# Layers 1 and 2 of a fused graph network: GpSimd steps cut in pieces, one mask comparison for two heads, roots and second norms queued later

## The chip, the cores and the metric

The kernel runs on one core of one Trainium2 chip. The time is device microseconds (us) of one execution; the smaller the better. TensorE (PE) multiplies matrices and loads a stationary operand before each product (PEld), VectorE (DVE) and ScalarE (ACT) do elementwise work, GpSimd (POOL) does elementwise work off to the side, and SyncE (SP) starts the transfers. Every engine has one queue of its own and takes its instructions strictly in that order, so an instruction that waits holds up all that stand behind it on the same engine.

## What is computed

Four graph layers on 3125 nodes of 128 features and 103,125 edges, each of the form x = layernorm(x + layer(x)). Layer 0 is a weighted neighbour sum with a ReLU. The two layers that the change touches are these:

```
# layer 1: attention over edges with 4 heads of 32 features
h = (x @ W).reshape(n, HEADS, C)
e = leaky_relu(a_s[src] + a_d[dst], 0.2); m = segment_max(e, dst); p = exp(e - m[dst])
out = segment_sum(h[src] * (p / segment_sum(p, dst)[dst]), dst)
out = out + gat_bias + x @ skip_W + skip_b
x = layernorm(x + layernorm(out) * ln_g + ln_b)
# layer 2: attention with one head
e = sum(Q[receiver] * K[sender]) * scale; w = exp(e - segment_max(e))
x = layernorm(x + (segment_sum(w * V[sender]) / segment_sum(w)) @ Wo)
```

Layer 3 is two mean-aggregating layers with a sigmoid.

## The kernel before, in words

**Dense counts.** The first third of the kernel turns the edge list into a dense table of edge counts (`ctd`, 25 blocks of 128 source nodes by 3200 destinations, bf16). All later layers are matrix products with that table. The 3125 nodes are 25 blocks of 128.

**Layer 1, the main loop.** The destinations are cut into four groups, `IG`, of 6, 7, 6 and 6 blocks; the heads are taken two at a time (`hp` is 0 or 2); inside, `c` runs over the 25 source blocks. One (group, hp, c) is an item; there are 200. I call the 25 items of one (group, hp) a half. For an item, TensorE needs the counts `ct` (a transfer of one source block by n destination blocks) and for each of two heads a mask `cm`: the counts where the leaky ReLU of the edge score is on its positive branch, zero elsewhere. For each of the n destination blocks there is one product with the counts (L1297) and one per head with the mask (L1302), 3n in all, summed over c in n PSUM banks.

**The masks.** `masks` (L1262 on) makes a mask in one of two ways. One in five is one VectorE instruction (L1280), a comparison times the counts with a float32 input. The others are a ScalarE activation into a tile `fm` (L1286: ReLU of the scaled score) and a VectorE minimum with the counts into `cm` (L1287). `fm` has 5 buffers, `cm` 8, `ct` 6. The masks of item x+2 are issued in step x.

**The order of the work around it.** A list of due times, filled by `later(k, f)`, places the rest: `step()` runs at the start of every item and issues whatever has come due, so "k items later" is a place in the engines' queues and not a time. The compiler's planner then orders each engine's queue by that order, its own estimate of costs, and free buffers. At the end of a half, `sums` adds up the three parts of each bank on VectorE (L1321), and GpSimd does four multiplications and additions on the result (L1327 to L1330); 4 items later (7 in the first group) `quotients` divides (L1337 to L1343). After both halves of a group, `finish1` is a chain: `norm1` (statistics on VectorE, L1021 to L1025, and the root on ScalarE, L1026), an item later `norm2` (scale, L1035, on ScalarE), three long GpSimd operations on all n blocks (L1082 to L1084: times ln_g, plus ln_b, plus x), 5 items after that the second `norm1`, an item later its `norm2`, and an item later `turns`: for each block, two items apart, a TensorE transposition (L1044), a copy, a product for layer 2 (L1048), and its evacuation (L1049 on ScalarE, L1050 on VectorE). This chain runs beside the next group's first half. When the destinations of a query group are done, `bound2` takes a maximum over all nodes by way of TensorE (L1002, L1013). `skips` adds the skip connection block by block, one per item, from item 2 of a group's first half (L1310, L1311).

**Layer 2.** Two query groups of 13 and 12 blocks by 25 sources: a score product (L1445), an exponential (L1448, ScalarE), a product with the counts (L1449, VectorE) and a sum (L1453, TensorE). The chain of the last group of layer 1 runs beside its first items with shorter distances, and `finish2` normalises after the first query group.

## Time and profile before

| what | value |
|---|---|
| time before, median of 3 runs | 1503.28 us (1501.07 to 1508.55) |
| the profiled execution's own time | 1507.44 us |
| its span in the trace | 1505.6 us |
| layer 1's main loop, first to last product | 540.3 to 948.7 us, 408.4 us |
| busy in that stretch: PE, PEld | 370.13, 353.98 us |
| busy in that stretch: DVE, ACT, POOL | 350.90, 323.23, 93.04 us |
| one `fm` activation (128x768), mean | 926 ns |
| one `cm` minimum (128x768), mean | 640 ns (median without GpSimd beside it 550 ns) |
| one `cm` comparison on VectorE alone (128x768), mean | 1079 ns |
| one long GpSimd operation (128x768), L1082 | 1989 ns mean, 1807 ns least |

The span is what the profiler sees from the first to the last instruction of the program; the device time of the same execution is 1.8 us longer. In the answers that list instructions in order of time, a row has the start, the duration (of several merged instructions, from the first start to the last end), the engine, the line, the operation, its output and inputs, and in brackets how long the engine had been idle before it and which instruction released it. In the table by stretches, "(x230)" is the number of instructions that began in it.

### The profile page before, as it was taken

To read this page: it belongs to the slowest core of one execution; us is meant where nothing else is said; L and a number is where in the kernel's file an instruction comes from. 1 tells how busy PE (TensorE), PEld (TensorE's weight loads), DVE (VectorE), ACT (ScalarE), POOL (GpSimd) and SP (SyncE) were. 2 spreads that over 40 slices of the span, in tenths; PEclk is the share of its full clock that TensorE was granted. 3 is DMA by queue.
4 is the path that set the end of the run, shared out by engine and by line. 5 is a ranking of instruction groups with operands and counts; after the bars stand their busy time and mean duration, and the time that the engine had idled before them with its cause. 6 is when DMAs were issued, how large, how long until landed. Compare 5 with 4: busy or idle time off the path is not lost.

```text
span 1505.6 us, 34986 instructions
## 1 busy us (share of the span) xinstructions
PE 1395.4 (93%) x14775; PEld 1227.3 (82%) x14775; DVE 978.8 (65%) x1575; ACT 914.3 (61%) x1865; POOL 128.9 (9%) x164
## 2 busy tenths in 40 slices
PE   3889999999998988998979989899999999999996
PEld 3889999999998878987978989677777774458996
DVE  4989899999991389898888879534464352012005
ACT  2978789888882489878867787454555331023005
POOL 1000000000000012132032113200000000000000
PEclk8999999999999999999999999999999999999998
DMA  7368789989887733443433534332222218512551
GB/s 206 96 179 226 198 221 242 234 213 230 238 218 221 222 115 114 125 124 113 135 90 112 142 88 117 115 121 70 69 60 81 71 47 309 200 53 114 197 174 46
DMA packets 209700, 223.91 MB, mean 149 GB/s; under 512 B 72956, under 2 KB 183339, under 8 KB 209277
## 3 DMA queue, kind: packets, MB, share of 16 engines
q1 hardware_dynamic: 208748, 218.51, 50.6%
q8 instruction: 117, 1.92, 0.5%
q0 software_dynamic: 400, 1.97, 0.4%
q10 hardware_dynamic: 385, 1.11, 0.2%
q14 instruction: 50, 0.41, 0.1%
HBM read 157.19 MB, written 64.36 MB: 147 GB/s over the span
## 4 chain that ended last, share of the span: by engine, by line
PE 72%; DVE 11%; ACT 8%; DMA 4%; issue 2%; POOL 2%; SPq 0%; ACTq 0%; DVEq 0%; POOLq 0%
PE wp L919 10%; PE acc L1302 9%; PE acc L1453 9%; PE s L1445 8%; PE acc L1553 7%; PE acc L1629 6%; PE acc L820 6%; PE acc L1297 5%; PE cp L911 3%; DVE cm L1287 3%; ACT wod L882 3%; PE left L820 2%; DMA cw<-wd 2%; ACT fm L1286 1%; DVE cm L1280 1%
## 5 line engine op out<-in xcount | busy, mean ns | idle before, releaser
L1302 PE MATMUL acc<-vp,cm 128*128 128x198 bf16 x2500 | 344.5, 252 | 8.2 <-DVE cm L1287 6.7
L1297 PE MATMUL acc<-vp,ct 128*128 128x204 bf16 x1250 | 317.1, 255 | 10.1 <-DVE vp L1205 4.5
L1286 ACT ACTIVATE fm<-adr,bas 128x768 bf16<-128x768 f32 (+1 forms) x320 | 287.2, 953 | 61.9 <-DVE cm L1287 60.1
L1302 PEld LDWEIGHTS <-cm 128*128 128x128 bf16 x2500 | 236.4, 98 | 25.2 <-DVE cm L1287 8.8
L919 PE MATMUL wp<-wod,ohc 128*128 128x128 bf16 x3768 | 239.6, 220 | 7.1 <-ACT cs L924 5.4
L919 PEld LDWEIGHTS <-ohc 128*128 128x128 bf16 x3768 | 220.9, 99 | 8.7 <-issue 8.3
L876 DVE TENSOR_TENSOR wod<-ohd,w 128x4096 bf16<-128x4096 bf16 (+2 forms) x122 | 221.4, 1867 | 0.4 <-PE wp L919 0.4
L1287 DVE TENSOR_TENSOR cm<-fm,ct 128x768 bf16<-128x768 bf16 (+1 forms) x320 | 202.6, 664 | 28.8 <-PE acc L1302 13.9
L882 ACT ACTIVATE wod<-ohd,wu 128x128 bf16<-128x128 bf16 x628 | 197.7, 397 | 0.0
L1449 DVE TENSOR_TENSOR e<-e,ct 128x416 f32<-128x416 f32 (+1 forms) x175 | 108.0, 623 | 110.4 <-ACT e L1448 102.8
L1448 ACT ACTIVATE e<-s,f_nm 128x416 f32<-128x416 f32 (+1 forms) x175 | 109.6, 633 | 103.1 <-PE s L1445 95.7
L1453 PEld LDWEIGHTS acc<-self__8043,e 128*128 128x128 f32 x1250 | 148.2, 192 | 19.8 <-issue 18.9
L820 PE MATMUL acc<-f_xw,cw 128*128 128x128 f32 x1000 | 147.8, 289 | 11.9 <-DMA cw<-wd 11.9
L1453 PE MATMUL acc<-self__8043,e 128*128 128x129 f32 x1250 | 148.5, 276 | 0.0
L1445 PE MATMUL s<-yT,f_xT 128*128 128x416 f32 (+1 forms) x350 | 143.1, 544 | 4.5 <-ACT rt L1425 2.6
L820 PEld LDWEIGHTS acc<-f_xw,cw 128*128 128x128 f32 x1000 | 127.7, 198 | 12.5 <-DMA cw<-wd 12.5
L1297 PEld LDWEIGHTS <-ct 128*128 128x128 bf16 x1250 | 122.1, 98 | 4.0 <-issue 2.7
L924 ACT CAST cs<-cp 128x500 bf16<-128x500 f32 x157 | 90.7, 578 | 39.5 <-PE cp L911 39.5
L1445 PEld LDWEIGHTS s<-yT,f_xT 128*128 128x128 f32 x350 | 62.5, 191 | 55.4 <-issue 40.7
L865 DVE TENSOR_TENSOR ohd<-kd,ramp 128x4096 bf16<-128x4096 bf16 (+1 forms) x41 | 90.1, 2200 | 20.3 <-PE cp L911 18.6
L930 ACT COPY ws<-wp 128x512 f32<-128x512 f32 x157 | 90.2, 579 | 20.9 <-PE wp L919 20.6
L911 PE MATMUL cp<-ohc,ohd 128*128 128x125 bf16 x1256 | 96.3, 220 | 3.7 <-ACT ws L930 3.5
(341 smaller groups left out, 1520.6 us busy)
## 6 DMA issues: line engine op xcount, KB each, us to landing
ct<-f_ctd SPq DMA_DIRECT2D x46, 800.0 KB
wd<-ws SPq DMA_DIRECT2D x39, 896.0 KB
cw<-wd SPq DMA_DIRECT2D x50, 640.0 KB
ct<-f_ctd SPq DMA_DIRECT2D x150, 192.0 KB
f_ctd<-cs SPq DMA_DIRECT2D x20, 1000.0 KB
ct<-f_ctd SPq DMA_DIRECT2D x50, 224.0 KB
ct<-f_ctd SPq DMA_DIRECT2D x25, 416.0 KB
ct<-f_ctd SPq DMA_DIRECT2D x25, 365.2 KB
```

The lines of the kernel that those rows point to most:

```text
L820: steps.append(lambda j=j, a=cw[:, j - h, :]: nc.tensor.matmul(accs[j // 4][:, j % 4, :], a, xw[:, i, :], start=False, stop=(i == NB - 1 a ...
L876: tip[s] = nc.vector.tensor_tensor(packed(f, ww), packed(ohd, ww), twos(w2[s])[:, ww], OP.mult)
L882: nc.scalar.activation(wod[2][:, BW + w, :], ohd[:, BW + w, :], AF.Copy, scale=w3[:, 1, at : at + 1])
L911: nc.tensor.matmul(cp[:, j, 0:KW], ohd[:, w, :], ohc[:, w, 0:KW], start=(j == 0 and q == 0), stop=(j == 3 and q == 1), skip_group_check=True,)
L919: made = nc.tensor.matmul(wp[:, j, :], ohc[:, w, :], wod[s][:, w, :], start=(j == 0 and q == 0 and s == 0), stop=(j == 3 and q == 1 and s ...
L1286: nc.scalar.activation(f[:, : n * P], at, AF.Relu, bias=bas[:, c, h : h + 1], scale=UP)
L1287: nc.vector.tensor_tensor(m[:, : n * P], f[:, : n * P], ct[:, : n * P], OP.min)
L1297: nc.tensor.matmul(out_(F1, PW), ct[:, k * P : (k + 1) * P], vp[:, c, hp : hp + 2, :, 2 * F1 : V1], start=(c == 0), stop=False, skip_group ...
L1302: nc.tensor.matmul(out_(0, 2 * F1)[:, j], ms[j][:, k * P : (k + 1) * P], vp[:, c, hp + j, :, 0 : 2 * F1], start=False, stop=(c == NB - 1 a ...
L1445: nc.tensor.matmul(s[:, :m], xT[:, c * P : (c + 1) * P], yT[:, i0 * P + a : i0 * P + a + m], start=True, stop=True)
L1448: nc.scalar.activation(e[:, a : a + m], s[:, :m], AF.Exp, bias=nm[:, q : q + 1], scale=scale)
L1453: nc.tensor.matmul(acc[k // 3][:, (k % 3) * (P + 1) : (k % 3 + 1) * (P + 1)], es[q, c][:, k * P : (k + 1) * P], vo[:, c, 0 : P + 1], start ...
```

## The change

Six things are done, all in layers 1 and 2.

1. The root (ScalarE's Sqrt) is taken out of `norm1` into `root`, and is issued one item after the statistics; `norm2` one item after that. This also holds for layer 2's `finish2`.
2. GpSimd's four steps after `sums`, issued at once before, are due 1, 2, 3 and 4 items later (a copy of the degrees 5), and `quotients` 6 (9) instead of 4 (7). The last half of the last group keeps them at once.
3. The three long GpSimd operations of `finish1` become six, on the first three and the remaining blocks, due an item apart. The second norm comes 8 items after the first scale instead of 5, `turns` 3 items after the second scale instead of 1. The last group issues the pieces at once, with the second norm 2 items later.
4. `bound2`'s transposition is due 3 items after its maximum and the rest 3 items after that, for the first query group. `skips` starts at item 5 instead of 2.
5. Both heads' masks of an item are in one tile `cm` (6 buffers, each twice as large; `fm` is gone). Where c % 5 == 2 both are made by VectorE alone. Otherwise ScalarE writes both activations into the tile and one VectorE minimum with the counts, repeated for the two heads, works on it in place.
6. The masks that are issued in the first item of a half get an edge: their VectorE instructions are queued behind the last L1321 of the half before.

```diff
@@ norm1
-        nc.scalar.activation(sd, sd, AF.Sqrt)
         return sp, mv, sd
+
+    def root(state):
+        nc.scalar.activation(state[2], state[2], AF.Sqrt)
@@ bound2
-        d = highest(sp, mq, 1)
-
-        def rest():
+        wait = 1 if q else 3
+
+        def rest(d):
...
-        later(1, rest)
+        def over():
+            d = highest(sp, mq, 1)
+            later(wait, lambda: rest(d))
+
+        if q:
+            over()
+        else:
+            later(wait, over)
@@ finish1
         def first_norm():
             keep["a"] = norm1(sp, r, i0, n)
-            later(gap[0], first_scale)
+            later(gap, lambda: root(keep["a"]))
+            later(gap + 1, first_scale)
+
+        def affine(m):
+
+            j = slice(m // 3 * 3, 3 if m < 3 else n)
+            nj = j.stop - j.start
+            row_ = (g_row, b_row)[m % 3][:, None, :].to_broadcast([P, nj, P]) if m % 3 < 2 else xs[:, j]
+            nc.gpsimd.tensor_tensor(rs[:, j], rs[:, j], row_, OP.mult if m % 3 == 0 else OP.add)
 
         def first_scale():
             norm2(keep["a"], r, r, i0, n)
-            nc.gpsimd.tensor_tensor(rs, rs, g_row[:, None, :].to_broadcast([P, n, P]), OP.mult)
-            nc.gpsimd.tensor_tensor(rs, rs, b_row[:, None, :].to_broadcast([P, n, P]), OP.add)
-            nc.gpsimd.tensor_tensor(rs, rs, xs, OP.add)
-            later(gap[1], second_norm)
+
+            for m in range(6):
+                if g == len(IG) - 1:
+                    affine(m)
+                else:
+                    later(1 + m, lambda m=m: affine(m))
+            later(2 if g == len(IG) - 1 else 8, second_norm)
 
         def second_norm():
             keep["b"] = norm1(sp, r, i0, n)
-            later(gap[0], second_scale)
+            later(gap, lambda: root(keep["b"]))
+            later(gap + 1, second_scale)
...
-            later(gap[0], lambda: turns(0))
+            later(1 if g == len(IG) - 1 else 3, lambda: turns(0))
@@ masks
-        mp = st.enter_context(tc.tile_pool(name="f_mp1", bufs=8))
+        mp = st.enter_context(tc.tile_pool(name="f_mp1", bufs=6))
...
-            ms = []
-            for h in (hp, hp + 1):
-                at = adrs[g, hp][:, h - hp, : n * P]
-                m = mp.tile([P, 7 * P], BF16, name="cm")
-                if (2 * c + h) % 5 == 0:
-                    nc.vector.scalar_tensor_tensor(
-                        m[:, : n * P], at, nas[:, c, h : h + 1], ct[:, : n * P], OP.is_gt, OP.mult
-                    )
-                else:
-
-                    f = mp.tile([P, 7 * P], BF16, name="fm", bufs=5)
-                    nc.scalar.activation(f[:, : n * P], at, AF.Relu, bias=bas[:, c, h : h + 1], scale=UP)
-                    nc.vector.tensor_tensor(m[:, : n * P], f[:, : n * P], ct[:, : n * P], OP.min)
-                ms.append(m)
-            ready_[g, hp, c] = (ct, ms)
+            m = mp.tile([P, 2, 7 * P], BF16, name="cm")
+            if c % 5 == 2:
+                for j in range(2):
+                    made = nc.vector.scalar_tensor_tensor(
+                        m[:, j, : n * P], adrs[g, hp][:, j, : n * P], nas[:, c, hp + j : hp + j + 1], ct[:, : n * P],
+                        OP.is_gt, OP.mult,
+                    )
+            else:
+
+                for j in range(2):
+                    nc.scalar.activation(
+                        m[:, j, : n * P], adrs[g, hp][:, j, : n * P], AF.Relu, bias=bas[:, c, hp + j : hp + j + 1], scale=UP
+                    )
+                made = nc.vector.tensor_tensor(
+                    m[:, :, : n * P], m[:, :, : n * P], ct[:, None, : n * P].to_broadcast([P, 2, n * P]), OP.min
+                )
+            ready_[g, hp, c] = (ct, m)
+            return made
@@ sums
-            nc.gpsimd.tensor_tensor(lo, lo, fbb[1], OP.mult)
-            nc.gpsimd.tensor_tensor(hi, hi, fbb[0], OP.mult)
-            nc.gpsimd.tensor_tensor(hi, hi, lo, OP.add)
-            nc.gpsimd.tensor_tensor(hi, hi, self_[:, i0 : i0 + n, hp : hp + 2, :], OP.add)
+            last = pool is lp
+            for k, (o, y, op) in enumerate((
+                (lo, fbb[1], OP.mult), (hi, fbb[0], OP.mult), (hi, lo, OP.add),
+                (hi, self_[:, i0 : i0 + n, hp : hp + 2, :], OP.add),
+            )):
+                if last:
+                    nc.gpsimd.tensor_tensor(o, o, y, op)
+                else:
+                    later(1 + k, lambda o=o, y=y, op=op: nc.gpsimd.tensor_tensor(o, o, y, op))
...
-            later(1 if last else 4 if g else 7, quotients)
+            later(1 if last else 6 if g else 9, quotients)
@@ the items of layer 1
-            if c == (2 if g else 0) and hp == (0 if g else H - 2):
+            if c == (5 if g else 0) and hp == (0 if g else H - 2):
                 later(0, lambda: skips(i0, i0 + n))
...
-                masks(*items[y_])
+                with ExitStack() as q_:
+                    if c == 0 and summed[0]:
+                        q_.enter_context(tc.issue_after(summed[0].ins))
+                    masks(*items[y_])
@@ finish2
                 keep[h] = norm1(ends[-1], r, *halves[h])
-                later(1, lambda: two(h))
+                later(1, lambda: root(keep[h]))
+                later(2, lambda: two(h))
```

More of the change, by code (lines that the diff above doesn't have):

```diff
@@ L1302, in products @@
                 nc.tensor.matmul(
-                    out_(0, 2 * F1)[:, j], ms[j][:, k * P : (k + 1) * P], vp[:, c, hp + j, :, 0 : 2 * F1],
+                    out_(0, 2 * F1)[:, j], ms[:, j, k * P : (k + 1) * P], vp[:, c, hp + j, :, 0 : 2 * F1],
                     start=False, stop=(c == NB - 1 and j == 1), skip_group_check=True,
@@ L1320, in sums @@
             for k in range(n):
-                nc.vector.tensor_reduce(
+                summed[0] = nc.vector.tensor_reduce(
                     nz[:, k], acc[k][:, 0 : 2 * HW].rearrange("p (h s c) -> p h c s", s=3, c=PW), AX.X, OP.add
@@ L1326, in sums @@
             fbb = [fb[:, s, i0 : i0 + n, hp : hp + 2, None].to_broadcast([P, n, 2, F1]) for s in range(2)]
-            nc.gpsimd.tensor_tensor(lo, lo, fbb[1], OP.mult)
-            nc.gpsimd.tensor_tensor(hi, hi, fbb[0], OP.mult)
-            nc.gpsimd.tensor_tensor(hi, hi, lo, OP.add)
-            nc.gpsimd.tensor_tensor(hi, hi, self_[:, i0 : i0 + n, hp : hp + 2, :], OP.add)
+            last = pool is lp
[7 more added lines that the diff above has]
+                    later(1 + k, lambda o=o, y=y, op=op: nc.gpsimd.tensor_tensor(o, o, y, op))
             if hp == 0:
-                nc.gpsimd.tensor_copy(deg[:, i0 : i0 + n], nz[:, :, 0, 2 * F1])
-            last = pool is lp
+                later(5, lambda: nc.gpsimd.tensor_copy(deg[:, i0 : i0 + n], nz[:, :, 0, 2 * F1]))
             def quotients():
@@ L1344, in quotients @@
                 if hp == H - 2:
-                    later(1 if last else 3, lambda: finish1(ends[-1], g, (1, 1) if last else (1, 5)))
-            later(1 if last else 4 if g else 7, quotients)
+                    later(1 if last else 3, lambda: finish1(ends[-1], g, 1))
+            later(1 if last else 6 if g else 9, quotients)
         ends.append(sp)
+        summed = [None]
         acc = None
```

## The prediction, made before the change was run

> **What bounds the kernel now.** I read the page's shares first, then the table by stretches, then who waited for whom, then the time order around the worst places.
>
> ```profile
> PE 1395.4 (93%) x14775; PEld 1227.3 (82%) x14775; DVE 978.8 (65%) x1575; ACT 914.3 (61%) x1865; POOL 128.9 (9%) x164
> PEclk8999999999999999999999999999999999999998
> ```
>
> TensorE is the bound over the whole; what can be won in layer 1 is only time in which it doesn't run at its pace. The table by stretches gives the pace and the room:
>
> ```profile
> 720.00:740.00 20.00, 20.00 (x230) 20.00 (x229) 14.88 (x23) 17.61 (x19) 0.00 (x0) 1.00 0.47 128
> 780.00:800.00 20.00, 13.57 (x121) 12.44 (x122) 13.94 (x40) 14.59 (x27) 2.29 (x2) 0.83 0.20 54
> 880.00:900.00 20.00, 15.87 (x135) 14.26 (x136) 14.37 (x39) 16.49 (x31) 1.37 (x1) 0.83 0.26 70
> ...
> 540.30:948.70 408.40, 370.13 (x3907) 353.98 (x3908) 350.90 (x701) 323.23 (x451) 93.04 (x83) 0.97 0.40 113
> ```
>
> The columns are PE, PEld, DVE, ACT, POOL busy, then the granted clock. Undisturbed, 230 products run in 20 us, 87 ns each: an item of 18 takes 1.57 us, of 21 1.83 us. In layer 1 PEld is busy 353.98 of 408.40 us, so at most 54 us can be won. I counted the loads item by item and subtracted pace and the other lines' loads: 52 us too long in all. Of these, 20.6 lie in three places (around 686, 780 and 883, two items each: 3.8, 9.6 and 7.2), 18.1 in the first seven items of the seven later halves, 10.4 in the first half, and the rest is scattered. Two of the three places are the two stretches with a clock of 0.83. Most items in the second part of a half are at pace to 0.1 us.
>
> What happens at 780, in order of time:
>
> ```profile
> 775.57 2.09 POOL L1082 TENSOR_TENSOR f_xw<-f_xw,f_g_row 128x896 f32<-128x896 f32 x1 [10.50 <-ACT f_xw L1035]
> 776.28 4.14 DVE L1287 TENSOR_TENSOR cm<-fm,ct 128x768 bf16<-128x768 bf16 x2 [1.24 <-ACT fm L1286]
> 777.74 2.27 POOL L1083 TENSOR_TENSOR f_xw<-f_xw,f_b_row 128x896 f32<-128x896 f32 x1
> 780.09 2.28 POOL L1084 TENSOR_TENSOR f_xw<-f_xw,f_x 128x896 f32<-128x896 f32 x1
> 782.40 1.45 DVE L1021 BATCH_NORM_STATS2 bs<-f_xw 128x6 f32<-128x128 f32 x7 [1.97 <-POOL f_xw L1084]
> 785.34 0.21 ACT L1026 ACTIVATE sd<-sd 128x7 f32<-128x7 f32 x1 [3.94 <-DVE sd L1025]
> 787.47 2.79 ACT L1035 ACTIVATE f_x<-f_xw,ms,sd 128x128 f32<-128x128 f32 x7
> 788.00 0.18 PEld L1044 LDWEIGHTS acc<-f_ident,f_x 128*128 128x128 f32 x1 [6.18 <-ACT f_x L1035]
> ```
>
> Three long GpSimd operations run in a row. Two minima take 4.14 us instead of some 1.0: each gets through only when a GpSimd operation has ended. VectorE then stands at the second norm's statistics until L1084 is done, ScalarE at the root behind them, and TensorE at the first transposition of `turns`. All are in-order queues, so masks, activations and products stand behind.
>
> The list of waits shows smaller ones of the same kind, `bound2`'s, and one in layer 2:
>
> ```profile
> PEld L1302 <- DVE cm L1287: 8.8, 9, 3.4
> PEld acc L1044 <- ACT f_x L1035: 6.2, 1, 6.2
> PEld few L1044 <- DVE self__8043 L1050: 5.5, 3, 2.7
> PEld s L1445 <- ACT rt L1425: 3.2, 1, 3.2
> ...
> PE few L1002 <- DVE mq L1058: 1.5, 1, 1.5
> PE acc L1013 <- DVE d_all L1007: 1.5, 1, 1.5
> ```
>
> **The change part by part.**
>
> *Second norm, roots, turns.* The chain from first scale to second norm gets 8 items (12.6 us at 1.57) instead of 5 (7.9). Its work: scales 2.8 (the row of L1035), then GpSimd 2.09 + 2.27 + 2.28 = 6.6 and gaps, 9.7 in all: too long for 5 items, inside 8. The root comes an item behind its statistics (7 L1021, 7 L1023, one L1025: 2.0 us with VectorE undisturbed), so ScalarE can do an item's activations instead of standing 3.9 us. Turns get three items, 4.7 us, for recip, scale and seven L1035 (0.3 + 2.8). The waits of 1.97, 3.94 and 6.18 should all go, and the low clock with them. What is late next: two norms of 2.0 us and the GpSimd pieces, now each some items apart, against a mask lead that I read as 3 to 3.5 us in undisturbed parts. I keep 1 us per place: 20.6 - 3 = 17.6 won. Ends: 0 (the stall moves) and 20.6.
>
> *Pieces.* An L1343 on 384 elements takes 0.95 us (954.81, VectorE quiet), an L1082 on 768 1.81 us: two pieces cost 0.1 us more than one long one, on an engine that is idle nine tenths of the time; no cost while the second norm has its slack of 2.9 us. GpSimd isn't paced by items: its queue holds nothing between the pieces, so they run back to back when their inputs are there. What changes is the grain: with VectorE let through between two operations, a piece of 1 us costs a mask 1 us, not 2.
>
> *Both masks in one minimum.* 160 of 1536 or 1792 elements replace 320. Undisturbed medians are 550 ns at 768 and 618 ns at 896, so 0.53 ns an element and 0.14 us fixed: 0.96 us for 1536. Against two of 0.55 that is 0.14 us less; in runs where rows overlap ("0.93 us x2" in the chain) some 0.03. So 5 to 22 us of VectorE over layer 1, beside TensorE in the steady part. The counts repeated over the middle dimension keep the two-per-cycle rate: L865 reads its `ramp` so and takes 2291 ns for 4096 elements, 0.56 ns each. The comparisons stay 80. An item's masks now wait for both activations, 0.85 us more than for one; the lead covers it. ScalarE writes into a tile that TensorE frees six items later instead of one that VectorE frees: more room, not less.
>
> *Boundaries of halves.* There VectorE does 6 or 7 sums (0.49 us apart), then runs behind with two items of masks ready while four GpSimd steps and two of `quotients` (5 to 8 us) take their turns. With one VectorE operation per GpSimd operation an item costs two GpSimd operations before and one after. Summing minima and comparisons that overlap GpSimd in layer 1 against their undisturbed medians gives 38.5 us lost beside 95 us of GpSimd, 0.40. One step of 0.9 to 1.2 us then costs 0.4 us per item: 0.96 + 0.4 is below 1.57. Of the 18.1 us in these items, `bound2` has 2.9 (its two waits above), which three items of distance remove. Of the other 15.2 I take half, 7 (ends 0 and 12). Item c = 2, two comparisons of 1.0 us, comes straight behind the sums by the new edge; that is in the half I leave. Skips, moved from item 2 to 5, leave this place to masks.
>
> The Trainium skill, page "SBUF — State Buffer", section "SBUF: two separate sides", says that VectorE with two SBUF inputs and GpSimd take a shared pair of ports in turn, as a lock that is kept for the whole instruction. The 4.14 us of two minima beside two GpSimd operations agree in kind. By the rule an item at a boundary would cost 0.96 + 0.95 to 1.2, or 1.9 to 2.2 us, above 1.57, shortening the operations would leave the sum locked the same, and the boundary term would be about 3 instead of 7, the total 4 smaller.
>
> *New costs.* `turns` now run from item 24 of a first half to item 12 of the second, across the boundary, in three groups. Each turn needs VectorE's or ScalarE's copy an item before the masks would. The price seen is 2.3 to 2.7 us for a turn that met the burst (L1044 waiting for L1050). I take 1 us per boundary, 3 in all; ends 0 and 8.
>
> *First half.* VectorE is full there (20.00 of 20.00 in 580 to 600); 20 joint minima save 0.03 to 0.14 each: 1.5 (ends 0.6 and 2.8).
>
> *Layer 2.* The 3.2 us at L1445 come from ScalarE standing at the second norm's root while the copy of the degrees waits behind. With the root an item later, I take 2 (ends 0 and 3.2). The last group's chain ends three or four items later (turns from item 9 instead of 6, the bound at 23 instead of 20); its blocks are needed from item 18 on and the second query group's bound at item 24, so it costs nothing with an item of 5.7 us in hand, and up to 3 us if that is missed. Transfers are the same in number and order; no SP issue moves.
>
> **Sum.** 17.6 + 2.9 + 7 + 1.5 + 2 - 3 = 28. The profiled execution has 1507.44, so 1479.4; the median is 4.2 us below that execution, so 1475; I say 1477.
>
> **The rivals.**
>
> *The stall moves.* VectorE, busy 351 of 408 us, is behind after statistics, pieces and sums alike; spacing them only spreads the wait. For: leads near zero after the GpSimd burst of 664 to 671, where no norm stood. Against: the steady items need 1.2 us of VectorE of 1.57. Price: a third of the first term (6), bound2 2.9, nothing at boundaries, -3: 6 us, so 1497.
>
> *Slower: turns across the boundary.* TensorE's queue is in order, so a transposition that waits for a scale or a copy behind the sums stops the products, and the sums stop too. For: L1044 waits are the largest of layer 1. Against: for groups of 6 two banks alternate. If the first turn in each of three groups costs the 9.6 us of 780 again, all 17.6 are gone; with 2.5 more for two later turns each (15), and the boundary gain of 7 gone, 28 - 17.6 - 7 - 12 is -9: 1512. It decides from about 9 us per boundary on.
>
> *Slower: the joint minimum at one element per cycle.* L1280 rises 1.06 ns per element between its two widths. At that rate a joint minimum takes 1.8 us, an item 1.85 us of VectorE instead of 1.2, above TensorE's 1.57: 200 items by 0.3, about 60 us: 1560. L865 speaks against it.
>
> **How the numbers follow.** My case 0.70 (its own range 1463 to 1492), the moving stall 0.14, turns 0.10, single rate 0.03, others 0.03. Half a percent, 7.5 us, is what this measurement can tell from no change. The moving stall lies half on either side of 1495.8: faster 0.77, same 0.11, slower 0.12. From 1460 to 1508 leaves out the slow rivals and a few percent below.
>
> **What would show it.** Right: no stretch of layer 1 with a clock of 0.83; L1044 waits under 1 us; the statistics no longer released by GpSimd; 160 minima of 0.95 us; main loop near 382 us. Wrong: L1302 waiting for the joint minimum throughout, or L1044 waits in the first items of second halves.

## The result, and the profile after

The changed kernel takes 1514.11 us (median of 11 runs, 1509.02 to 1517.02), the kernel before 1505.27 beside it (11 runs, 1501.07 to 1508.55): a ratio of 1.0052, 95% interval 1.0041 to 1.0062. The forecast was 1477; the change made the kernel 0.5% slower.

The two profiled executions differ by 1.6 us only (1509.02 against 1507.44), because the one of after is the fastest of its runs and the one of before among the slowest. So these two traces show only a part of the loss; where the rest of the 8.8 us lies can't be read from one execution of each. The granted clock of single executions varies too, over the same range in both kernels (0.973 to 0.986); the trace of before has 0.973 and the trace of after 0.986.

The page of after, shares and granted clock:

```profile
PE 1388.8 (92%) x14762; PEld 1218.5 (81%) x14775; DVE 949.0 (63%) x1415; ACT 910.7 (60%) x1865; POOL 134.3 (9%) x176
...
PEclk9999999999999999999999999999999999999998
```

The table by stretches (PE, PEld, DVE, ACT, POOL busy, granted clock, DMA share, GB/s):

```profile
539.10:951.30 412.20, 369.68 (x3907) 350.75 (x3908) 318.76 (x538) 320.51 (x451) 97.35 (x92) 0.98 0.39 112
...
770.00:790.00 20.00, 18.40 (x187) 17.76 (x186) 13.21 (x39) 15.32 (x23) 6.80 (x6) 0.91 0.37 99
780.00:800.00 20.00, 17.98 (x203) 17.49 (x202) 12.69 (x30) 15.57 (x28) 6.80 (x6) 1.00 0.40 107
...
880.00:900.00 20.00, 16.89 (x191) 16.41 (x189) 12.12 (x26) 16.28 (x26) 5.42 (x6) 1.00 0.38 100
```

VectorE is busy 32 us less in the main loop than before (318.76 against 350.90), the two stretches with a clock of 0.83 now have 1.00 (just before the first of them, from 770 to 790, it is 0.91), and the loop is 3.8 us longer (412.2 against 408.4). Less work and a slightly better clock (0.98 against 0.97 over the loop) did not shorten it. The waits show what did the opposite (in total, times, longest, for 520 to 960 us):

```profile
PEld L1326 <- DVE cm L1309: 26.4, 22, 2.9
DVE cm L1309 <- DMA ct<-f_ctd: 24.4, 29, 3.2
...
DVE bs L1021 <- POOL f_xw L1095: 16.8, 6, 3.6
...
DVE rz L1365 <- POOL nz L1359: 12.5, 7, 2.2
ACT sd L1029 <- DVE sd L1025: 12.3, 5, 5.0
...
DVE bs L1021 <- POOL f_xw L1371: 6.9, 4, 2.0
...
DVE rz L1365 <- POOL nz L1357: 1.5, 1, 1.5
...
PEld few L1013 <- DVE d_all L1007: 0.7, 1, 0.7
```

and the same in before:

```profile
DVE bs L1021 <- POOL f_xw L1084: 5.6, 2, 3.6
...
ACT sd L1026 <- DVE sd L1025: 4.2, 2, 3.9
...
DVE bs L1021 <- POOL f_xw L1343: 3.1, 3, 1.4
...
DVE rz L1337 <- POOL nz L1330: 1.5, 1, 1.5
```

VectorE stands for GpSimd 37.7 us (12.5 and another 1.5 at the divisions `rz`, 23.7 at the statistics `bs`); before it was 10.2. ScalarE stands at roots 12.3 us instead of 4.2. TensorE waits 26.4 us for the minima's masks, 8.8 before.

Where in the loop that lands, counted as in the prediction (time per item, less 87 ns a product, less the duration of the other lines' loads; an item runs from its first load to the next item's):

| too long, us | before | after |
|---|---|---|
| first half | 10.4 | 8.2 |
| first seven items of the seven later halves | 18.3 | 38.4 |
| their items 7 to 24 | 24.3 | 10.4 |
| all | 53.0 | 57.0 |

So the three long stalls of TensorE did go, all but a few us (the third row holds them), and the boundaries of the halves took back more than they gave. One boundary of after, VectorE and then GpSimd in order of time:

```profile
697.70 3.46 DVE L1345 TENSOR_REDUCE nz<-acc 128x134 f32<-128x402 f32 x7
701.09 2.92 DVE L1299 SCALAR_TENSOR_TENSOR cm<-adr,nas,ct 128x896 bf16<-128x896 f32 x2
703.93 1.86 DVE L1309 TENSOR_TENSOR cm<-cm,ct 128x1792 bf16<-128x1792 bf16 x1
707.99 0.17 DVE L1365 TENSOR_SCALAR rz<-nz 128x14 f32<-128x14 f32 x1 [2.20 <-POOL nz L1359]
...
708.50 1.07 DVE L1309 TENSOR_TENSOR cm<-cm,ct 128x1792 bf16<-128x1792 bf16 x1
```
```profile
701.25 3.59 POOL L1359 TENSOR_TENSOR nz<-nz,fb 128x462 f32<-128x462 f32 x2 [25.09 <-DVE nz L1345]
704.79 1.05 POOL L1361 COPY f_deg<-nz 128x7 f32<-128x7 f32 x1
705.80 1.00 POOL L1359 TENSOR_TENSOR nz<-nz 128x462 f32<-128x462 f32 x1
706.88 1.08 POOL L1359 TENSOR_TENSOR nz<-nz,self__8043 128x462 f32<-128x462 f32 x1
```

After the sums (L1345) VectorE makes the masks of two items only (two comparisons, one joint minimum). Then the division (L1365) stands in its queue, although the code asks for it 6 items after the sums, and waits 2.20 us until GpSimd's steps end at 707.96. The next minimum stands behind it and runs without a wait of its own once it gets its turn (708.50). Statistics of another group's second norm fare the same at 785 us:

```profile
784.79 0.68 DVE L1021 BATCH_NORM_STATS2 bs<-f_xw 128x6 f32<-128x128 f32 x3 [2.84 <-POOL f_xw L1095]
...
788.72 0.29 DVE L1021 BATCH_NORM_STATS2 bs<-f_xw 128x6 f32<-128x128 f32 x1 [3.03 <-POOL f_xw L1095]
```
```profile
783.76 1.00 POOL L1095 TENSOR_TENSOR f_xw<-f_xw,f_x 128x384 f32<-128x384 f32 x1
...
787.41 1.27 POOL L1095 TENSOR_TENSOR f_xw<-f_xw,f_x 128x512 f32<-128x512 f32 x1
```

VectorE waits for the third and for the sixth piece, 5.9 us together. Counting in VectorE's queue by how many items' masks (of 200) an instruction stands behind: the sums of the first group's second half stand behind 52, their division behind 54, and that group's second norm behind 66. Where the order of the code is kept, as in the run e1_pin below, the same two stand behind 61 and 74. In the kernel before, this norm stood behind 63 and 64; with the order of the code kept (e5_before_pin) it stands behind 68.

### The profile page after: what moved, and what is told of

Read it like the earlier page. It is cut to its first block, busy times and chain, and to the rows that moved or that the text cites. A ratio compares the mean times of both kernels' runs of the same rounds, so it can differ in the third digit from the quotient of the medians.

```text
span 1507.2 us, 34792 instructions
## 1 busy us (share of the span) xinstructions
PE 1388.8 (92%) x14762; PEld 1218.5 (81%) x14775; DVE 949.0 (63%) x1415; ACT 910.7 (60%) x1865; POOL 134.3 (9%) x176
## 4 chain that ended last, share of the span: by engine, by line
PE 69%; DVE 10%; ACT 8%; POOL 5%; DMA 4%; issue 3%; SPq 0%; DVEq 0%; ACTq 0%; POOLq 0%
PE wp L919 10%; PE acc L1485 9%; PE s L1477 8%; PE acc L1326 7%; PE acc L1586 7%; PE acc L1662 6%; PE acc L820 6%; PE acc L1321 4%; PE cp L911 3%; ACT wod L882 3%; POOL nz L1359 2%; DVE cm L1309 2%; PE left L820 2%; DMA cw<-wd 2%; ACT cm L1306 2%
## 5 line engine op out<-in xcount | busy, mean ns | idle before, releaser
L1326 PE MATMUL acc<-vp,cm 128*128 128x198 bf16 x2500 | 341.9, 251 | 22.7 <-DVE cm L1309 20.1
L1321 PE MATMUL acc<-vp,ct 128*128 128x204 bf16 x1250 | 313.9, 254 | 12.2 <-DVE nz L1345 4.2
L1306 ACT ACTIVATE cm<-adr,bas 128x768 bf16<-128x768 f32 (+1 forms) x320 | 283.6, 951 | 43.6 <-PE acc L1326 41.0
L1326 PEld LDWEIGHTS <-cm 128*128 128x128 bf16 x2500 | 233.2, 97 | 47.2 <-DVE cm L1309 26.4
L1309 DVE TENSOR_TENSOR cm<-cm,ct 128x1536 bf16<-128x1536 bf16 (+1 forms) x160 | 166.9, 1050 | 44.1 <-DMA ct<-f_ctd 24.4
L1321 PEld LDWEIGHTS <-ct 128*128 128x128 bf16 x1250 | 121.4, 97 | 4.2 <-issue 3.2
L930 ACT COPY ws<-wp 128x512 f32<-128x512 f32 x157 | 90.1, 577 | 20.1 <-PE wp L919 19.8
L865 DVE TENSOR_TENSOR ohd<-kd,ramp 128x4096 bf16<-128x4096 bf16 (+1 forms) x41 | 90.1, 2200 | 18.3 <-PE cp L911 17.4
```

What stands on the lines that cost most here:

```text
L1306: nc.scalar.activation(m[:, j, : n * P], adrs[g, hp][:, j, : n * P], AF.Relu, bias=bas[:, c, hp + j : hp + j + 1], scale=UP)
L1309: made = nc.vector.tensor_tensor(m[:, :, : n * P], m[:, :, : n * P], ct[:, None, : n * P].to_broadcast([P, 2, n * P]), OP.min)
L1321: nc.tensor.matmul(out_(F1, PW), ct[:, k * P : (k + 1) * P], vp[:, c, hp : hp + 2, :, 2 * F1 : V1], start=(c == 0), stop=False, skip_group ...
L1326: nc.tensor.matmul(out_(0, 2 * F1)[:, j], ms[:, j, k * P : (k + 1) * P], vp[:, c, hp + j, :, 0 : 2 * F1], start=False, stop=(c == NB - 1 a ...
```

## The experiments

My first theory (the queue theory of the expectations): the planner pulls VectorE's dependent steps forward in its queue, ahead of masks, so the distances in items are not kept, and VectorE stands for GpSimd. Rivals: the wider `cm` tiles and the counts' buffers (29.2 us of waits for `ct`, 24.4 of them at the minima), the joint minima, the turns across the boundary. "The edge" below means that what a step issues on VectorE is queued behind the last mask issued before it. All numbers of the runs are in the table; "waits" is VectorE's standing for GpSimd at divisions and statistics between 520 and 960 us. Boundaries (the first seven items of the seven later halves) and rest (their items 7 to 24) are, as above, the time that is too long; loop, boundaries, rest and waits are of one profiled execution each.

Each ratio is against runs of the kernel before on the same chip (medians 1503.86 to 1505.37); loop is first to last product.

| run | median us | ratio, 95% interval | loop us | first half | boundaries | rest | waits us |
|---|---|---|---|---|---|---|---|
| before | 1505.27 | 1 | 408.3 | 10.4 | 18.3 | 24.3 | 10.2 |
| after | 1514.11 | 1.0052 (1.0041 to 1.0062) | 412.1 | 8.2 | 38.4 | 10.4 | 37.7 |
| e1_pin | 1488.31 | 0.9904 (0.9884 to 0.9925) | 390.5 | 9.3 | 18.8 | 7.9 | 6.3 |
| e2_ct7 | 1504.31 | 1.0011 (0.9999 to 1.0022) | 407.9 | 9.7 | 33.9 | 10.0 | 34.3 |
| e3_masks | 1516.75 | 1.0086 (1.0057 to 1.0115) | 421.2 | 9.9 | 30.4 | 25.4 | 27.7 |
| e4_order | 1502.95 | 0.9993 (0.9984 to 1.0003) | 406.2 | 10.1 | 26.7 | 14.5 | 16.4 |
| e5_before_pin | 1503.82 | 0.9999 (0.9984 to 1.0014) | 408.5 | 8.4 | 17.5 | 27.1 | 8.3 |
| e6_order_pin | 1489.71 | 0.9892 (0.9864 to 0.9921) | 393.2 | 8.3 | 22.5 | 7.3 | 4.9 |
| e7_pin_ct7 | 1486.06 | 0.9869 (0.9840 to 0.9897) | 391.0 | 10.9 | 15.3 | 9.8 | 6.3 |
| e8_masks_pin | 1500.04 | 0.9968 (0.9951 to 0.9984) | 404.1 | 10.7 | 11.4 | 26.7 | 8.2 |
| e9_pin_l2 | 1478.93 | 0.9827 (0.9794 to 0.9860) | 390.1 | 9.0 | 16.4 | 9.6 | 1.4 |
| e10_pin_act | 1488.36 | 0.9895 (0.9866 to 0.9923) | 389.7 | 11.1 | 15.1 | 8.8 | 6.3 |
| e11_turns_late | 1483.79 | 0.9867 (0.9841 to 0.9894) | 387.8 | 10.7 | 14.1 | 8.2 | 6.3 |
| e12_pin_norms | 1498.04 | 0.9955 (0.9939 to 0.9971) | 400.7 | 9.7 | 31.7 | 4.5 | 17.3 |
| e13_pin_div | 1496.29 | 0.9944 (0.9928 to 0.9961) | 400.8 | 9.6 | 20.4 | 15.7 | 18.2 |
| e14_far | 1512.42 | 1.0056 (1.0035 to 1.0078) | 417.6 | 9.7 | 43.6 | 8.5 | 31.2 |
| e15_l2_turns | 1478.02 | 0.9822 (0.9806 to 0.9839) | 389.1 | 10.6 | 15.6 | 8.2 | 1.4 |
| e16_cmp1 | 1510.01 | 1.0032 (1.0016 to 1.0049) | 413.9 | 12.8 | 23.3 | 22.8 | 23.4 |
| e17_l2_cmp1 | 1481.89 | 0.9837 (0.9800 to 0.9874) | 393.3 | 8.9 | 22.2 | 7.3 | 0.0 |

### The edge alone, and the counts' buffers alone

e1_pin, the changed kernel with the edge:

```diff
-            step()
+            with ExitStack() as q_:
+                if pinned:
+                    q_.enter_context(tc.issue_after(pinned[-1].ins))
+                step()
...
-                    masks(*items[y_])
+                    pinned.append(masks(*items[y_]))
```

> The changed kernel, with one edge more: the VectorE instructions that a step issues are queued behind the last mask issued before that step, so that the planner can't put them earlier. Queue theory (VectorE's divisions and statistics were placed four to six items before their due step and wait there for GpSimd): VectorE's waits for GpSimd in layer 1's main loop, 38 us in the changed kernel (18.7 + 6.9 at L1021, 14.0 at L1365 less some outside), fall below 8, TensorE's waits for joint minima from 26 to below 10, the main loop from 412 to about 390 to 397, the time from 1514 to 1490 to 1499. Counts theory (masks wait for the transfers of counts, 29 us): waits for counts stay at 25 to 30, the time stays within 4 us of 1514. Turns theory (turns across the boundary of halves): the second halves keep their excess of 10, 4 and 5 us, time 1505 to 1514.

e2_ct7, the changed kernel with another buffer for the counts:

```diff
-        cp = st.enter_context(tc.tile_pool(name="f_cp1", bufs=6))
+        cp = st.enter_context(tc.tile_pool(name="f_cp1", bufs=7))
```

> The changed kernel with 7 buffers of counts instead of 6 (more don't fit), all else as it is. Counts theory: the masks' waits for counts fall from 29 to below 15 us and the time by 5 to 10 us, to 1504 to 1509. Queue theory and turns theory: the waits for counts may fall, but they lie mostly where the masks have a lead of 4 to 5 us; the time stays within 3 us of 1514.

Measured: the edge turns 0.5% slower into 1.0% faster; the loop falls by 21.6 us, the boundaries from 38.4 to 18.8, TensorE's waits for the minima's masks from 26.4 to 10.6 us. The queue theory had forecast this to within 2 us of its ranges. The buffer takes the waits for counts from 29.2 to 1.1 us and wins about 6 us by the ratios, 4.2 us of it seen in the loop; VectorE's standing for GpSimd stays (34.3). So the waits for counts had a price of their own in the changed kernel, as the counts theory said; the queue theory's forecast for this run, within 3 us of 1514, missed. With the edge the waits for counts are as long as without (28.1) and harm little: removing them there (e7_pin_ct7) is not to be told from nothing (the intervals of the two ratios overlap). The same boundary with the edge, VectorE in order of time:

```profile
688.46 3.47 DVE L1345 TENSOR_REDUCE nz<-acc 128x134 f32<-128x402 f32 x7
691.84 2.92 DVE L1299 SCALAR_TENSOR_TENSOR cm<-adr,nas,ct 128x896 bf16<-128x896 f32 x2
694.68 1.86 DVE L1309 TENSOR_TENSOR cm<-cm,ct 128x1792 bf16<-128x1792 bf16 x1
...
696.67 1.84 DVE L1309 TENSOR_TENSOR cm<-cm,ct 128x1792 bf16<-128x1792 bf16 x1
698.44 1.97 DVE L1299 SCALAR_TENSOR_TENSOR cm<-adr,nas,ct 128x896 bf16<-128x896 f32 x1
700.34 1.08 DVE L1309 TENSOR_TENSOR cm<-cm,ct 128x1792 bf16<-128x1792 bf16 x1
...
701.54 1.08 DVE L1309 TENSOR_TENSOR cm<-cm,ct 128x1792 bf16<-128x1792 bf16 x1
702.53 1.14 DVE L1299 SCALAR_TENSOR_TENSOR cm<-adr,nas,ct 128x896 bf16<-128x896 f32 x1
703.60 0.17 DVE L1365 TENSOR_SCALAR rz<-nz 128x14 f32<-128x14 f32 x1
```

Six items of masks (four comparisons, four minima) now lie between sums and division, and the division waits for nothing: it runs 11.7 us after the sums' end instead of 6.8, and the loop is shorter for it.

### Which part of the change costs what, with and without the edge

e3_masks is the kernel before with only the joint masks (parts 5 and 6 of the change):

```diff
+            m = mp.tile([P, 2, 7 * P], BF16, name="cm")
+            if c % 5 == 2:
...
+                made = nc.vector.tensor_tensor(
+                    m[:, :, : n * P], m[:, :, : n * P], ct[:, None, : n * P].to_broadcast([P, 2, n * P]), OP.min
+                )
```

e4_order is the changed kernel with the masks of before in separate tiles, so the distances and pieces without part 5. Part 6, the edge behind the sums, stands in both runs; none has joint masks without it:

```diff
+                    f = mp.tile([P, 7 * P], BF16, name="fm", bufs=5)
+                    nc.scalar.activation(f[:, : n * P], at, AF.Relu, bias=bas[:, c, h : h + 1], scale=UP)
+                    nc.vector.tensor_tensor(m[:, : n * P], f[:, : n * P], ct[:, : n * P], OP.min)
```

> The kernel before with the joint masks alone (one tile of 6 buffers, one minimum for two heads, both comparisons at c % 5 == 2, the edge behind the sums); all distances as before. Queue theory: it is the joint masks that make the planner place the divisions 2 items and the statistics 4 to 8 items behind the sums, so this kernel has VectorE's waits for GpSimd at 30 us or more although VectorE is busy some 30 us less, and is no faster than before: 1503 to 1520. Turns theory: turns are where they were, so the gain of the masks shows: 1485 to 1497. Counts theory: waits for counts of 20 to 30 us as in the changed kernel, 1505 to 1515.

> The changed kernel with the masks of before (two tiles, two minima, fm of 5 and cm of 8 buffers); all distances, pieces, roots and the edge as changed. Queue theory: the planner puts divisions and statistics within an item or two of where they stood in the kernel before, pieces and roots help a little at the second norm: 1495 to 1505. Turns theory: the turns across the boundary cost by themselves: 1507 to 1516. Counts theory: no waits for counts over 5 us, the gain of the distances shows: 1485 to 1497.

e5_before_pin, e6_order_pin and e8_masks_pin are the kernel before, e4_order and e3_masks with the edge of e1_pin; e7_pin_ct7 is e1_pin with the seven buffers of e2_ct7.

> The kernel before with the edge alone: VectorE's instructions of a step stay behind the last mask issued before that step. Nothing else is changed. Queue theory: in the kernel before the planner put divisions and statistics nearly where they were due, so the edge changes little: 1498 to 1507. Rival (the edge is what wins, whatever the distances and masks): 1485 to 1495.

> The changed distances, pieces and roots with the masks of before (two minima an item) and the edge behind the last mask. Queue theory: the distances now hold on VectorE's queue, the second norm no longer waits for GpSimd and the turns not for the norm; VectorE still has its 30 us more of work at the boundaries: 1490 to 1498. Rival (the joint masks carry the gain of the pinned kernel): 1500 to 1506.

> The changed kernel with the edge behind the last mask and 7 buffers of counts. If the waits for counts (28 us on VectorE's queue in the pinned kernel) cost TensorE time there, they fall to below 5 and the time to 1480 to 1485. If they lie where the masks have a lead, the loop stays at 390 us; the time can still fall by up to 5 us, since the stage before layer 1 ended 4 us earlier in the run with 7 buffers: 1483 to 1490.

> The kernel before with the joint masks and the edge behind the last mask; distances as before. Queue theory: the 13 us that the joint masks alone cost go (divisions and statistics are behind their masks again), and the lighter VectorE wins some, but the second norm still stands 5 items behind the first scale and waits for GpSimd's long operations as in the kernel before: 1492 to 1502. Rival (joint masks cost by themselves, by waits for counts or for the second activation): 1508 to 1518.

| median us | without the edge | with the edge |
|---|---|---|
| neither part | 1503.9 | 1503.8 |
| joint masks only | 1516.8 | 1500.0 |
| distances and pieces only | 1503.0 | 1489.7 |
| both | 1514.1 | 1488.3 |

These runs come from more than one chip; the ratios in the large table, each against the same chip, give the same picture. What follows. The edge by itself does nothing for the kernel before. The distances shorten the long stalls (rest 24.3 to 14.5, with the edge 7.3), but without the edge they give most of the gain back at the boundaries (18.3 to 26.7). The joint masks alone make the boundaries 12.1 us worse (30.4) and leave the stalls. The two boundary losses add up: 18.3 + 8.4 + 12.1 = 38.8, and both together measure 38.4. With the edge the joint masks cost nothing any more: at the old distances they win 0.3% (e8_masks_pin against e5_before_pin, boundaries 11.4 against 17.5), at the new ones nothing that can be told (e1_pin against e6_order_pin). The distances win 1.1% with the edge and two minima, 0.6% with the edge and joint ones. So what the joint masks cost is an effect of the queue's order, not of the minimum's speed: a joint minimum is 958 ns in the median, two of before were 553 ns each. What the distances win, they win in the rest: at the boundaries they cost 5.0 us (17.5 to 22.5) and 7.4 us (11.4 to 18.8) even with the edge.

### Divisions or statistics

e12_pin_norms has the edge on the two `norm1` of `finish1` only:

```diff
+            with ExitStack() as q_:
+                if g < len(IG) - 1:
+                    q_.enter_context(tc.issue_after(pinned[-1].ins))
+                keep["b"] = norm1(sp, r, i0, n)
```

e13_pin_div has it on the maximum and the reciprocal of `quotients` only:

```diff
+                with ExitStack() as q_:
+                    if not last:
+                        q_.enter_context(tc.issue_after(pinned[-1].ins))
+                    nc.vector.tensor_scalar(rz, hi[:, :, :, C], 1e-38, None, OP.max)
+                    nc.vector.reciprocal(rz, rz)
```

> The changed kernel with the edge on the statistics of the two norms alone; the divisions of the quotients, the scales' reciprocals and the copies stay where the planner puts them. If the statistics, hoisted ahead of masks, are the whole loss (they wait 16.8 and 6.9 us for GpSimd), the time is 1488 to 1492, as with the edge on everything; if the divisions (12.5 us of waits) carry half of it, 1497 to 1504; if neither is the cause, 1512 or more.

> The changed kernel with the edge on the two VectorE instructions of the quotients (maximum and reciprocal of the sums' weights) alone; statistics and copies stay where the planner puts them. If the loss is the sum of statistics (16 us by the run with the edge on them) and divisions, this run wins the other 10 and stands at 1502 to 1506. If the divisions only hand their wait on to the statistics, it stands at 1511 to 1515. If one of the two places is enough to lead the rest back, 1490 to 1498.

The waits of e12_pin_norms, where line numbers are up to 7 higher:

```profile
DVE rz L1372 <- POOL nz L1366: 12.4, 7, 2.2
...
DVE bs L1022 <- POOL f_xw L1099: 2.0, 1, 2.0
...
DVE bs L1022 <- POOL f_xw L1378: 1.4, 1, 1.4
```

and of e13_pin_div:

```profile
DVE bs L1021 <- POOL f_xw L1095: 11.1, 4, 3.9
...
DVE bs L1021 <- POOL f_xw L1374: 5.6, 4, 1.8
...
DVE rz L1368 <- POOL nz L1357: 1.5, 1, 1.5
```

Each edge removes its own waits and leaves the other's. Both are at fault, in different places: the divisions at the boundaries (38.4 to 20.4), the statistics in the later items (10.4 to 4.5) and for 6.7 us of the boundaries. By the ratios the statistics give 1.0% and the divisions 1.1%, the edge on everything 1.5%: they overlap. With the divisions alone in place the rest rises to 15.7; I read that as the chain behind them, which starts later and meets its statistics there, but no run shows it by itself. e13_pin_div won more than the 10 us that were left after e12_pin_norms; the two are not a sum.

### Does the distance set the place?

e14_far, the changed kernel without the edge:

```diff
-            later(2 if g == len(IG) - 1 else 8, second_norm)
+            later(2 if g == len(IG) - 1 else 11, second_norm)
...
-            later(1 if last else 6 if g else 9, quotients)
+            later(1 if last else 9 if g else 12, quotients)
```

> The changed kernel, no edge, with the quotients 9 items behind the sums instead of 6 (12 instead of 9 in the first group) and the second norm 11 items behind the first scale instead of 8. Theory 'a distance is no place in VectorE's queue, the planner puts a step where it holds its inputs ready': the divisions stay 2 items behind the sums, and the time is that of the change, 1510 to 1517. Rival 'the planner moves a step ahead by a fixed 4 to 6 items, so larger distances make up for it': the waits for GpSimd go from 36 us to under 10, and the time is 1488 to 1497.

```profile
696.22 3.47 DVE L1345 TENSOR_REDUCE nz<-acc 128x134 f32<-128x402 f32 x7
699.60 2.92 DVE L1299 SCALAR_TENSOR_TENSOR cm<-adr,nas,ct 128x896 bf16<-128x896 f32 x2
702.45 1.86 DVE L1309 TENSOR_TENSOR cm<-cm,ct 128x1792 bf16<-128x1792 bf16 x1
706.52 0.18 DVE L1365 TENSOR_SCALAR rz<-nz 128x14 f32<-128x14 f32 x1 [2.21 <-POOL nz L1359]
```

Three items more in the code, and the division stands in the same place with the same wait; the first group's second norm, too, stands behind 66 as in after. The ratio is that of the change. A longer distance does not buy a later place.

e16_cmp1 moves the comparisons instead, out of the first item behind the sums:

```diff
-            if c % 5 == 2:
+            if c % 5 == 1:
```

> The changed kernel, no edge, with both heads' comparisons in the items 1, 6, 11, 16 and 21 instead of 2, 7, 12, 17 and 22 (their number is the same). Theory 'two comparisons straight behind the sums are what turns the planner's order': the divisions then stand 4 to 6 items behind the sums in VectorE's queue instead of 2, their waits for GpSimd (12.5 us) go, the first seven items of the later halves lose 20 to 27 us instead of 38, and the time is 1494 to 1503. Rival 'the joint minima themselves do it': 1510 to 1517 as with the change.

```profile
DVE bs L1021 <- POOL f_xw L1095: 15.7, 6, 3.8
...
DVE bs L1021 <- POOL f_xw L1371: 3.5, 2, 2.0
...
DVE rz L1365 <- POOL nz L1359: 2.7, 2, 1.8
```

Half of it came. In the three later groups the divisions move to their due places (in VectorE's queue behind the masks of 83, 108, 133, 158 and 183 items, six after the sums, instead of 79, 104, 128, 154 and 179); in the first group they stand 6 and 4 items after the sums where the code has 9. Their waits go from 12.5 to 2.7 us; the boundaries lose 23.3. But the statistics still wait 19.2 us, the rest rises to 22.8, the first half to 12.8, and the time is 1510, not under 1503. So where the comparisons lie among the items sends the division forward; that this is how the joint masks hurt is shown for the place, not for the time. What the planner's estimate sees there was not tried.

### What is left

e9_pin_l2 is e7_pin_ct7 with an edge in layer 2 too: a step's VectorE and ScalarE instructions behind the last exponential and product of the scores issued before.

```diff
+                tops = (
+                    nc.scalar.activation(e[:, a : a + m], s[:, :m], AF.Exp, bias=nm[:, q : q + 1], scale=scale),
+                    nc.vector.tensor_tensor(e[:, a : a + m], e[:, a : a + m], ct[:, a : a + m], OP.mult),
+                )
...
+            with ExitStack() as q_:
+                for o in tops:
+                    q_.enter_context(tc.issue_after(o.ins))
+                step()
```

> The changed kernel with the edge on VectorE's steps in layer 1, seven buffers for the counts, and in layer 2 each step's VectorE and ScalarE instructions behind the last exponential and product of the scores issued before. Theory 'the layer 2 head is also a matter of queue places' (ScalarE stands at the root of the last second norm, in front of the exponentials): the gap before the first scores, 3.39 us, falls under 1 us, and the time is 1483 to 1484. Rival 'the head waits for the chain of the last group itself': the gap stays, or moves to the bound of the second query group, and the time is 1486 or more.

ScalarE at the last group's second root, in after

```profile
976.31 1.28 ACT L1029 ACT_TABLE_LOAD   x1 [5.68 <-DVE sd L1025]
```

and in e9_pin_l2

```profile
948.27 2.70 ACT L1485 ACTIVATE e<-s,f_nm 128x416 f32<-128x416 f32 x4 [2.99 <-PE s L1481]
950.99 1.28 ACT L1029 ACT_TABLE_LOAD   x1
```

ScalarE no longer stands 5.68 us at the root in front of exponentials. TensorE's gaps of 1.81 and 3.39 us at the head of layer 2 are gone; from the end of layer 1's last product to TensorE's end it is 536.4 us, 541.6 in after. At 1478.93 us (ratio 0.9827) this is 1.7% faster than the kernel before, and by the ratios some 6 us faster than e7_pin_ct7, where 2 to 3 were expected. The edge holds VectorE's and ScalarE's steps together; no run parts them.

e10_pin_act is e7_pin_ct7 with layer 1's ScalarE steps behind the last activation as well:

```diff
-                    nc.scalar.activation(
+                    relu[0] = nc.scalar.activation(
...
+                    q_.enter_context(tc.issue_after(relu[0].ins))
```

e11_turns_late and e15_l2_turns move the turns of e7_pin_ct7 and e9_pin_l2 from 3 to 9 items behind the second scale, clear of the boundary. e17_l2_cmp1 is e9_pin_l2 with the line of e16_cmp1, `c % 5 == 1`.

```diff
-            later(1 if g == len(IG) - 1 else 3, lambda: turns(0))
+            later(1 if g == len(IG) - 1 else 9, lambda: turns(0))
```

> The same kernel (edge on VectorE's steps, seven buffers for the counts) with the steps' ScalarE instructions of layer 1 (roots, scales and copies) also behind the last activation issued. Theory 'ScalarE's queue has the same fault' (it stands 11.1 us at roots whose statistics are not done): these waits fall under 3 us and the time is 1481 to 1484. Rival 'ScalarE's standing is slack that the masks' lead covers': 1486, within 1.5 either way.

> The same kernel (edge, seven buffers) with the turns nine items behind the second scale instead of three, so that they start in item 5 of the second half, clear of the boundary. Theory 'turns across the boundary are what is left there' (the rival of the prediction): the first seven items of the three second halves lose 2 to 3 us each now, and would come to pace; time 1480 to 1483. Rival 'they cost nothing that masks would not': 1486, within 2 either way.

> The edge in layers 1 and 2, seven buffers for the counts, and the turns nine items behind the second scale instead of three. If the turns at the boundary are what is left there, 2 to 6 us less than with the turns at three: 1473 to 1477. If they cost nothing that masks would not, 1479, within 2.

> The best version so far (edges in layers 1 and 2, seven buffers for the counts) with the comparisons in items 1, 6, 11, 16 and 21. If two comparisons behind the sums also cost VectorE's lead at the boundary (2.9 us for two beside GpSimd, where two minima of other items would take less), 2 to 5 us are won: 1474 to 1477. If the edge has already taken what there is: 1479, within 2.

ScalarE's standing at roots stays at 11.0 us in e10_pin_act and nothing is won: an edge behind the activations does not remove these waits, so the run doesn't show what they cost. (e1_pin has 13.2 us of them and after 12.3, so they are not what makes after slower.) The turns cost next to nothing at the boundary: ratios 0.9869 and 0.9867, 0.9827 and 0.9822, and the first seven items of the last three second halves go from 10.5 to 9.5 us when the turns leave. Moving the comparisons wins nothing once the edge is there (0.9837 against 0.9827, outside both forecasts of the time by 1 us). Some 15 us remain at the boundaries in the best version; none of the runs names their cause.

## Why the prediction was wrong, point by point

**The step that failed** is the first sentence of the term for norms and turns, "The chain from first scale to second norm gets 8 items (12.6 us at 1.57) instead of 5 (7.9)", and with it the term for the boundaries, which rests on the division coming 6 items after the sums, as the code has it. Both read a distance in items as a place in VectorE's queue. The description of the kernel itself said that a planner orders each queue by its own estimates after the code has set the order; I did not ask where it would put the instructions. It put the divisions 1 or 2 items behind the sums and the second norms 6 to 8 items ahead of where they stand with the edge, and VectorE stands for GpSimd 37.7 us instead of 10.2. With the edge that makes the distances hold, the same change is 1.0% faster than the kernel before; with the counts' buffer and the edge in layer 2, 1.7% (1478.93, close to the 1477 forecast, in part for reasons that were not in the sum).

**Second norm, roots, turns, -17.6.** Half of the mechanism was right: TensorE's three stalls go, the clock at these places rises, and of the three waits that "should all go" the one of a transposition for ScalarE's scale (6.18) goes. The other two grew: VectorE's at the second norm's statistics from 5.6 to 16.8 us in all, ScalarE's at roots from 4.2 to 12.3. Items 7 to 24 of the later halves win 13.9 (e4_order 9.8), and 16.4 with the edge.

**Boundaries, -7, and `bound2`, -2.9.** Together -9.9 forecast, +20.1 measured (18.3 to 38.4); this is nearly the whole error in the trace. `bound2`'s waits did fall, from 3.0 to 1.1 us, the rest got worse, and even with the edge the boundaries stand at 18.8, no better than before: with the queue's order held, spacing cost 5 to 7 us there, and no run shows why (the turns are about 1 of it).

**Pieces.** Right: they run back to back at 1.0 us for 384 elements, and their due times, an item apart, don't pace them (three pieces between 781.57 and 784.76). That was said as a comfort; it also meant that spacing them by items does nothing.

**Joint minimum.** Right in price: 0.96 us forecast, 0.958 measured, so the rival of one element per cycle is out. VectorE's busy time fell by 32 us where 5 to 22 were forecast, and the value was still small: with the edge, joint minima win 0.3% at the old distances, and at the new ones e6_order_pin without and e1_pin with them have the same ratio within their intervals.

**First half, -1.5:** 2.2 won in the trace of after, while the runs with the edge stand at 8.3 to 11.1: not told from scatter. **Turns, +3:** about 1 by e11_turns_late. **Layer 2, -2:** not won; the root an item later in the code still waited in front of the exponentials, 5.68 us, and the gap went from 2.55 to 3.39. With the edge on VectorE's and ScalarE's steps (e9_pin_l2) that wait and the gap are gone.

**The rivals.** "Turns across the boundary" had the number (1512) and not the mechanism: there is no large wait at a transposition (1.2 us in all at L1046), so the match is luck. Its sum is off as well: three stalls of 9.6 us are 28.8, not 17.6, which would make it about 1523. "The stall moves" had the mechanism in part, VectorE behind after sums and statistics, but gave the boundaries no loss. No rival asked whether the order in the code is the order in the queue.

**The lock.** The Trainium skill, page "SBUF — State Buffer", section "SBUF: two separate sides", describes a port pair that VectorE and GpSimd hold in turn for a whole instruction. At the boundary shown above a GpSimd step takes 1.8 us beside VectorE and 1.00 alone, a joint minimum 1.86 beside it and 1.09 alone: 1.86 of the sum of 2.09. There the two nearly add up, nearer to the page than to my 0.40, which was a mean over all positions. Instruction by instruction the ends alternate: VectorE at 702.23, 704.00 and 705.79, GpSimd at 703.06 and 704.84.

## What to carry to other kernels

Where a planner orders the queues, a delay written in loop steps is a wish. Before forecasting the gain of "k items later", find the instruction's place in its engine's queue, count what stands between it and its input, and if it must come later, tie it behind a named instruction. Here short instructions with a late input, hoisted ahead of work that was ready, cost more than was won on the long ones that the profile shows on top. And a change that shortens one engine's work can turn the planner's order elsewhere (the joint masks did): measure the parts of such a change with the order held fixed.

## What was not expected of the hardware

VectorE's busy time was no guide. It is 318.8 us in the loop of after and 335.4 in e1_pin, whose loop is 21.6 us shorter: masks that run beside GpSimd take longer (1.86 instead of 1.09 us) and still beat masks that stand behind a wait. The granted clock is no guide either as it stands in two traces: it rises from 0.973 to 0.986 over the whole span from before to after, but single executions of each kernel spread over just this range. Among the eleven of after a lower clock goes with a longer time (0.973 to 0.975: 1513.3 to 1517.0 us; 0.985 and 0.986: 1509.0 to 1510.3), which may be one reason why the two profiled executions lie so close; among those of before no such order shows (1500.63 us at 0.977, 1505.37 at 0.983). What a low clock costs here stays open.
